# A four-layer convolution network on one core: image halves cut left and right instead of upper and lower, and a ninth-tap pass of 496 columns

## The chip, the cores and the metric

The kernel runs on one core of one Trainium2 chip. The metric is the device time of one execution in microseconds. The kernel before was run three times, 2502.79 to 2504.33 us, with a median of 2503.82 us. One more execution was profiled; times inside the kernel come from that one.

## The reference

The input `x` has the shape (4, 32, 32, 16): batch, rows, columns, channels. Four layers run one after the other, each as `x = x + layer(group_norm(x))`. Layers 0, 1 and 3 are of the kind that matters here:

```python
first = jnp.einsum('ijyx,byxc->bijc', Msq, inputs)
kern = jnp.transpose(G, (0, 1, 5, 4, 2, 3)).reshape(h * w * f, c, 3, 3)
shifted = lax.conv_general_dilated(x_nchw, kern, (1, 1), 'SAME')   # an own 3x3 kernel for each output pixel (i, j)
diff = jax.nn.relu(inputs[:, None, None, :, :, :] - shifted)
second = jnp.einsum('ijyx,bijyxc->bijc', Wsq, diff)
return first - second
```

So for each of the 1024 pixels (i, j) and each of 16 filters the whole 32 x 32 image is convolved with a 3x3x16 kernel of its own (zero padding at the borders), the result is subtracted from the image, clipped at zero and summed with weights. Layer 2 is another one (running maxima over intervals and small matrix products); the change does not touch it.

## The kernel before

**Tiles.** A convolution is a matrix product over 9 taps x 16 channels = 144 rows. The weights of 128 output pixels are the stationary operand, an image is the moving one. The batch is two groups `g` of two images. A *phase* is one group in one of the three convolution layers, so there are six; a phase has 8 *chunks* `t` of 128 pixels, a chunk has 16 filters `f` and 2 images `b`, so there are 6 x 8 x 32 = 1536 *steps*. A *unit* is 4 filters of one chunk: 8 steps share one load of weights.

**Row tiles.** An image is cut into two halves `h` of 512 pixels. Half 0 goes through rows 0 to 63 of the matrix engine, half 1 through rows 64 to 127, at the same time, and they write two PSUM banks. 64 rows hold four taps of 16 channels, so two row blocks (`s` = 0, 1) hold eight taps; the ninth tap, the one a row below and a column to the right, has a block of its own (`im9` with the weights `W9`; the 64 rows hold it four times for the precision scheme). Values are split in a high and a low part (`iy`, `iz`, `iyz`, weights `WU`, `WL`, `WD`), to reach fp32 precision with matmuls in fp32r. A step has 7 *passes*: two with `iy`, two with `iz`, two with `iyz`, and one with `im9`; a pass is a pair of matmuls of 64 rows x 128 columns of weights and 512 columns of image, one on each row tile. `products` (line 581) issues them (line 590). The first 16 steps (`u < PLAIN`) are simpler: two passes in full fp32 straight from the tile `raw`, which count as four in the trace, and the `im9` pass.

**Order.** All queues are written out by hand. `conv_layer` goes through the steps: `first_part` of step i (four passes, then ScalarE scales the bank pair, line 620), then `second_part` of step i-1 (three passes, then VectorE's clip, weighting and sum in one instruction, line 636). Four bank pairs rotate. Between the steps two generators insert other work: `prep_parts` makes the weight parts of the next units (VectorE, ScalarE, GpSimd, then two copies on SyncE's queue from one half of the partitions to the other, line 239, which the second pass of a unit's first step is the first to need), and `behind(phase)` makes the input of the next phase: group norm, then `before_conv` (line 340 on). There the normalized image `xn` is transposed into `xt`, written to the DRAM tile `xs` with a border of zeros (line 352, four transfers), and read back as shifted copies, one for each tap and half, into `raw` (line 361, 24 transfers); then it is split into `iy`, `iz`, `iyz`, `im9` (`split`, `halve`, `difference`). SyncE's queue carries the weight loads `raw<-in_g` (line 107), `WT<-in_w` (113), the copies `parts<-parts` (239) and these transfers, in one order.

**Layout before.** Half `h` is the upper or lower 16 rows of 32 columns; the padded image is 34 wide. The ninth tap reads a row below: the last row of the lower half reads zeros, in the upper half it does not.

**Start.** The first phase gets its shifted images from the host (`xi`, line 143). `kept` (line 746 on) holds for each row of the engine and each border whether it is a tap that looks outside; `normal` normalizes `raw`, and `sides` (line 796) then sets the borders to zero by multiplying with `kept`.

Of the kernel before, what the change touches and what calls it, by code (L numbers as in the profile page):

```python
# [8 lines left out]
F32 = mybir.dt.float32  # L9
# [6 lines left out]
P = 128  # L16
# [5 lines left out]
NP = H * H  # L22
NT = NP // P
HP = H + 2
NPP = HP * HP
HI = H // 2
PITCH = HI * HP
NH = HI * H
RUN = (HI - 1) * HP + H
ROWS = P // H  # L30
FU = 4
NU = C // FU
# [9 lines left out]
def net_kernel(ctx: ExitStack, tc: tile.TileContext, x, xq, xi, convs, iv_w, iv_b, out):  # L42
# [73 lines left out]

    raw = const.tile([P, 3, GB, PITCH], F32, name="raw")
    const.tile([P, 32], F32, name="pad")  # L120
# [4 lines left out]
    const.tile([P, 112], F32, name="pad_parts")  # L125


    F0 = 2
# [46 lines left out]
            dst, src, mask[:, 0:1], dst.bitcast(F32), op0=ALU.mult, op1=ALU.add  # L175
        )

    xs = [dram.tile([GC, NPP], F32, name=f"xs{g}") for g in range(NG)]
    zero = const.tile([P, HP], F32, name="zero")
    xt = [const.tile([P, NT, HP], F32, name=f"xt{g}") for g in range(NG)]  # L180

    def zeros(g):

        nc.gpsimd.memset(xt[g], 0.0)
        for y in (0, HP - 1):
            nc.gpsimd.dma_start(xs[g][:, y * HP : (y + 1) * HP], zero[:GC])

    def image(v, x):
        return v.rearrange("... (y x) -> ... y x", x=x)[..., :H]

    def upper(src, n, name):

        t = work.tile([P, 2, NH], F32, tag="upper", bufs=2, name=f"upper_{name}")[:, :n]
        t = t.rearrange("p s (y x) -> p s y x", x=src.shape[3])
        nc.vector.tensor_scalar(  # L195
            t.bitcast(I32), src.bitcast(I32), HIGH, None, op0=ALU.bitwise_and
        )
        return t.rearrange("p s y x -> p s (y x)")
# [58 lines left out]

    def split(eng, g, b, name, pause=IDLE):

        high = upper(image(raw[:, :2, b], HP), 2, f"x{name}{b}")  # L260
        yield 1
        for s in range(2):
            eng.tensor_tensor(
                image(iz[g][:, s, b], H), image(raw[:, s, b], HP), image(high[:, s], H), ALU.subtract
            )
            yield pause
            nc.scalar.activation(iy[g][:, s, b], high[:, s], AF.Copy, scale=EPS)  # L267
# [72 lines left out]
    def before_conv(g, layer):  # L340
        xn = work.tile([P, NT, GC], F32, tag="xn", bufs=2, name=f"xn_{g}_{layer}")
        xns[g] = xn
        yield from group_norm(g, f"c{g}{layer}", xn, 1 if layer == 2 else 4)

        nc.vector.transpose(
            xt[g][:, :, 1 : 1 + H], xn
        )
        inner = xs[g][:, HP : HP + H * HP].rearrange("p (t r n) -> p r t n", r=ROWS, n=HP)  # L350
        for r in range(ROWS):
            nc.sync.dma_start(inner[:, r], xt[g][GC * r : GC * (r + 1)])
        yield 2
        xsv = xs[g].rearrange("(b c) n -> c b n", b=GB)
        for slot, row, tap in [(tap // 4, tap % 4, tap) for tap in range(8)] + [
            (2, row, 8) for row in range(4)
        ]:
            for h in range(2):
                off = (HI * h + tap // 3) * HP + tap % 3
                r0 = 64 * h + C * row  # L360
                nc.sync.dma_start(
                    raw[r0 : r0 + C, slot ^ h if slot < 2 else 2, :, :RUN], xsv[:, :, off : off + RUN]
                )
            yield 1
        yield 6 if layer == 2 else 12
        for b in range(GB):
            yield from split(nc.gpsimd, g, b, f"{g}{layer}")
            yield IDLE
            halve(image(im9[g][:, b], H), image(raw[:, 2, b], HP), low_x)
            for s in range(2):  # L370
                difference(nc.gpsimd, g, b, s)
            yield 3
            halve_rest(image(im9[g][:, b], H), image(raw[:, 2, b], HP), low_x)
            yield 1

    def load_first_terms(layer):
# [204 lines left out]
        yield 1  # L581


    def products(ps, pairs, first):


        for k, (w, v) in enumerate(pairs):
            for h in range(2):
                r = slice(64 * h, 64 * h + 64)
                nc.tensor.matmul(  # L590
                    ps[:, h, :],
                    lhsT=w[r],
                    rhs=v[r],
                    start=first and k == 0,
                    stop=k == len(pairs) - 1,
                    skip_group_check=not first,
                )

    def first_part(step):
        phase, t, f, b = step  # L600
        g = phases[phase][0]
        n = phase * NT + t
        u = n * NU + f // FU
        ps = bank_pair(f"pc_{n}_{f}_{b}")
        if u < PLAIN:
            products(
                ps,
                [(raws[u][:, s, f % FU], image(raw[:, s, b], HP)) for s in range(2)]
                + [(units[u][3][:, f % FU], im9[g][:, b])],
                True,  # L610
            )
# [8 lines left out]
        nc.scalar.activation(ps, ps, AF.Copy, scale=1.0 + EPS)  # L620
        return ps

    def second_part(step, ps):
# [5 lines left out]
        if u >= PLAIN:  # L629
            WU, WL, WD, W9 = (w[..., f % FU, :] for w in units[u])  # L630
            products(
                ps, [(WD[:, s], iyz[g][:, s, b]) for s in range(2)] + [(W9, im9[g][:, b])], False
            )
        col = b * C + f
        junk = work.tile([P, NP], F32, tag="junk", name=f"junk_{n}_{col}")
# [92 lines left out]
    for b in range(GB):  # L728
# [6 lines left out]
    )  # L735

    outside = {
        "left0": (rows[:, 0, 0::3], rows[:, 1, 2:3]), "right0": (rows[:, 0, 2:3], rows[:, 1, 1:2]),
        "top0": (rows[:, 0, 0:3],), "bottom0": (rows[:, 1, 2:4],),
        "left1": (rows[:, 0, 2:3], rows[:, 1, 0::3]), "right1": (rows[:, 0, 1:2], rows[:, 1, 2:3]),  # L740
    }
    kept = const.tile([P, len(outside) + 4], F32, name="kept")
    keep = {}
    for k, (name, views) in enumerate(outside.items()):
        keep[name] = kept[:, k : k + 1]
        nc.vector.tensor_reduce(keep[name], views[0], axis=AX.X, op=ALU.add)
        if len(views) > 1:
            also = kept[:, len(outside) + k % 4 : len(outside) + k % 4 + 1]
            nc.vector.tensor_reduce(also, views[1], axis=AX.X, op=ALU.add)
            nc.vector.tensor_tensor(keep[name], keep[name], also, ALU.add)  # L750
    kept = kept[:, : len(outside)]
# [43 lines left out]

    def sides(eng, b, slot):

        v = raw[:, slot, b].rearrange("p (y x) -> p y x", x=HP)
        if slot == 2:
            eng.memset(v[:, :, H - 1 : H], 0.0)  # L800
            eng.memset(v[64:, HI - 1, :H], 0.0)
        for side, at in (
            ("left", v[:, :, 0]), ("right", v[:, :, H - 1]),
            ("top", v[:, 0, :H]), ("bottom", v[:, HI - 1, :H]),
        ):
            if f"{side}{slot}" in keep:
                eng.tensor_scalar_mul(at, at, keep[f"{side}{slot}"])  # L807
# [15 lines left out]
    normal(nc.vector, 0, 1)  # L823
    sides(nc.vector, 0, 1)
    sides(nc.gpsimd, 0, 2)
    halve(image(im9[0][:, 0], H), image(raw[:, 2, 0], HP), low_x)
    halve_rest(image(im9[0][:, 0], H), image(raw[:, 2, 0], HP), low_x)
    prep_plain(0, F0, FU, nc.vector)

    def rest_of_start():  # L830

        nc.sync.dma_start(X[0], x[0])
        load_raw(2)
        load_raw(3)
        prep_plain_rest(0, F0, FU)
        for slot in (0, 1, 2):
            normal(nc.vector, 1, slot)
            sides(nc.vector, 1, slot)
        halve(image(im9[0][:, 1], H), image(raw[:, 2, 1], HP), low_x)
        prep_plain(1)  # L840
        prep(2)
        yield 1
        halve_rest(image(im9[0][:, 1], H), image(raw[:, 2, 1], HP), low_x)
# [12 lines left out]
        yield from group_norm(0, "c00", xns[0], 4)  # L856
# [82 lines left out]
```

## Time and profile before

| | |
|---|---|
| three runs, median | 2503.82 us |
| the profiled execution, whole | 2503.48 us |
| its span (first to last instruction) | 2501.8 us |
| granted clock of the matrix engine | 1.0 |
| TensorE matmul (PE) busy | 99% of the span |
| weight load (PEld) busy | 83% |
| VectorE (DVE) busy | 83% |
| ScalarE (ACT) busy | 75% |
| GpSimd (POOL) busy | 44% |
| DMA engines busy | about half of the span |

Everything outside the span is 2503.48 - 2501.8 = 1.7 us. A line of a group reads: line of the kernel, engine, operation, output<-inputs, shapes, count | busy time in us, mean duration of one in ns | idle time of the engine just before them, and what ended most of it. PE is the matmul itself, PEld the weight load, SPq SyncE's queue of transfers. "64\*128 64x512" is a matmul with 64 rows and 128 columns of weights and 512 columns of moving data. Matmuls are pipelined, so the duration of one is longer than the distance from one to the next.

### The profile page before, as it was taken

The page shows a single profiled execution, that of the slowest core. Times are in us where ns is not written, and L with a number is a line of the kernel's source. Part 1 is how long each engine was busy: PE and PEld are TensorE (multiplying, and loading weights), DVE is VectorE, ACT ScalarE, POOL GpSimd, SP SyncE. Part 2 cuts the span into 40 slices and gives each one's busy share as a digit, 9 for nine tenths or more (in the row PEclk, how much of TensorE's full clock was granted, in tenths as well). Part 3 has the DMA queues.
Part 4 walks back from the last instruction along what each step waited for, and adds up shares of the span by engine and source line. Part 5 has one row for each costly group of instructions (what it writes and reads, how often), then busy time and mean ns, then how long its engine had stood idle before and what let it go on. Part 6 is the DMA issues. An engine that isn't in the chain of part 4 may idle for free.

```text
span 2501.8 us, 56663 instructions
## 1 busy us (share of the span) xinstructions
PE 2485.7 (99%) x21906; PEld 2077.8 (83%) x21906; DVE 2078.6 (83%) x3620; ACT 1884.8 (75%) x2181; POOL 1102.3 (44%) x991
## 2 busy tenths in 40 slices
PE   8999999999999999999999999999999999999999
PEld 5899888888888887888888888888889888888887
DVE  8888777888888887888888988888889887788887
ACT  4777777787777777777777777787777777777776
POOL 3445333454343435433345555454646444333332
PEclk9999999999999999999999999999999999999999
DMA  5556444465444664544454444554444467354442
GB/s 174 185 148 171 121 136 140 118 171 140 133 139 134 200 163 123 140 133 133 133 144 136 136 119 138 144 159 133 124 137 137 133 167 203 112 144 136 135 136 54
DMA packets 81182, 353.80 MB, mean 141 GB/s; under 512 B 18448, under 2 KB 20368, under 8 KB 80144
## 3 DMA queue, kind: packets, MB, share of 16 engines
q1 hardware_dynamic: 79920, 349.57, 49.8%
q8 instruction: 172, 2.82, 0.5%
q14 instruction: 98, 0.80, 0.1%
q10 hardware_dynamic: 864, 0.58, 0.1%
q0 software_dynamic: 128, 0.02, 0.0%
HBM read 199.19 MB, written 0.98 MB: 80 GB/s over the span
## 4 chain that ended last, share of the span: by engine, by line
PE 97%; DMA 1%; DVE 1%; issue 1%; ACT 1%; SPq 0%; POOL 0%; ACTq 0%; DVEq 0%; POOLq 0%
PE pc L590 95%; DMA parts<-parts 1%; PE pf L389 1%; DVE junk L636 0%; ACT pc L620 0%; PE ps_l L512 0%; PE ps_r L525 0%; DVE tables L472 0%; ACT parts L232 0%; ACT iy L267 0%; ACT L325 0%; ACT L555 0%; SPq L239 0%; DVE raw L807 0%; PE ps_y L576 0%
## 5 line engine op out<-in xcount | busy, mean ns | idle before, releaser
L636 DVE SCALAR_TENSOR_TENSOR junk<-pc,WT 128x1024 f32<-128x1024 f32 x1536 | 1879.9, 1224 | 398.6 <-PE pc L590 351.0
L620 ACT ACTIVATE pc<-pc 128x1024 f32<-128x1024 f32 x1520 | 1531.9, 1008 | 583.5 <-PE pc L590 549.8
L590 PE MATMUL pc<-iy,parts 64*128 64x512 f32 x6080 | 955.7, 388 | 1.3 <-DMA parts<-parts 1.0
L590 PE MATMUL pc<-iyz,parts 64*128 64x512 f32 x6080 | 953.6, 387 | 2.2 <-ACT pc L620 2.1
L590 PE MATMUL pc<-iz,parts 64*128 64x512 f32 x6080 | 952.7, 387 | 0.0
L590 PEld LDWEIGHTS pc<-iy,parts 64*128 64x128 f32 x6080 | 589.6, 184 | 112.6 <-issue 4.4
L590 PEld LDWEIGHTS pc<-iyz,parts 64*128 64x128 f32 x6080 | 589.2, 184 | 111.1 <-ACT pc L620 6.3
L229 POOL TENSOR_TENSOR parts<-raw,upper_w 128x512 fp32r<-128x512 f32 x190 | 246.0, 1295 | 985.5 <-PE pc L590 817.0
L590 PEld LDWEIGHTS pc<-iz,parts 64*128 64x128 f32 x6080 | 591.1, 184 | 105.1
L590 PE MATMUL pc<-im,W 64*128 64x512 f32 x3072 | 620.0, 391 | 0.0
L590 PEld LDWEIGHTS pc<-im,W 64*128 64x128 f32 x3072 | 301.0, 184 | 56.7 <-issue 3.6
L230 POOL TENSOR_TENSOR W<-W,raw 128x512 fp32r<-128x512 f32 x190 | 247.8, 1304 | 1.9 <-ACT W L171 1.6
L233 POOL TENSOR_TENSOR parts<-parts 128x512 fp32r<-128x512 f32 x190 | 247.2, 1301 | 2.5 <-ACT parts L228 2.4
L206 POOL TENSOR_TENSOR raw<-raw,ident 128x512 f32<-128x512 f32 x190 | 201.9, 1063 | 54.6 <-DMA raw<-in_g 49.3
L171 ACT ACTIVATE W<-raw,low_w 128x512 fp32r<-128x512 f32 x190 | 136.1, 716 | 1.0 <-DMA raw<-in_g 1.0
L636 DVE DVE_READ_ACCUMULATOR junk<-pc,WT 128x1 f32 x1536 | 127.8, 83 | 0.0
L228 ACT ACTIVATE parts<-upper_w 128x512 fp32r<-128x512 f32 x190 | 118.7, 625 | 3.4 <-DVE upper_w L195 3.3
L232 ACT CAST parts<-upper_w 128x512 fp32r<-128x512 f32 x190 | 116.8, 615 | 0.0
L195 DVE TENSOR_SCALAR upper_w<-raw 128x512 int32<-128x512 int32 x190 | 82.2, 433 | 0.2
L651 POOL TENSOR_SCALAR acc<-acc 128x32 f32<-128x32 f32 x40 | 11.5, 288 | 159.3 <-DVE junk L636 155.2
L544 POOL TENSOR_TENSOR tables<-ft_b,rt 128x1089 f32<-128x1089 f32 x16 | 37.7, 2356 | 0.1
L544 POOL TENSOR_TENSOR tables<-ft_a,rt 128x1089 f32<-128x1089 f32 x16 | 37.6, 2350 | 0.0
(140 smaller groups left out, 393.5 us busy)
## 6 DMA issues: line engine op xcount, KB each, us to landing
raw<-in_g SPq DMA_DIRECT2D x190, 768.0 KB, 7.0
parts<-parts SPq DMA_DIRECT2D x380, 384.0 KB, 4.9
WT<-in_w SPq DMA_DIRECT2D x48, 512.0 KB, 4.8
MT<-in_mt SPq DMA_DIRECT2D x6, 2048.0 KB, 14.3
raw<-xs SPq DMA_DIRECT2D x120, 67.8 KB, 2.5
raw<-in_xi SPq DMA_DIRECT2D x3, 271.0 KB, 4.6
raw<-in_xi SPq DMA_DIRECT2D x1, 813.0 KB, 7.0
xs<-xt SPq DMA_DIRECT2D x20, 34.0 KB, 2.1
```

The source lines that it names most:

```text
L171: nc.scalar.activation(dst, src, AF.Copy, scale=mask[:, 1:2])
L195: nc.vector.tensor_scalar(t.bitcast(I32), src.bitcast(I32), HIGH, None, op0=ALU.bitwise_and)
L206: eng.tensor_tensor(raws[u][:, s, at:to], raws[u][:, s, at:to], pick[s][:, f0 + at : f0 + to].unsqueeze(2).to_broadcast([P, to - at, P]), ...
L228: nc.scalar.activation(WD, high, AF.Copy, scale=-EPS)
L229: nc.gpsimd.tensor_tensor(WL, w8, high, ALU.subtract)
L230: nc.gpsimd.tensor_tensor(W9, W9.bitcast(F32), src[:, 2], ALU.add)
L232: nc.scalar.copy(WU, high)
L233: nc.gpsimd.tensor_tensor(WD, WD.bitcast(F32), WL.bitcast(F32), ALU.add)
L544: nc.gpsimd.tensor_tensor(t, ft[:, i, :].unsqueeze(1).to_broadcast([P, T1, T1]), rt, ALU.add,)
L590: nc.tensor.matmul(ps[:, h, :], lhsT=w[r], rhs=v[r], start=first and k == 0, stop=k == len(pairs) - 1, skip_group_check=not first,)
L620: nc.scalar.activation(ps, ps, AF.Copy, scale=1.0 + EPS)
L636: nc.vector.scalar_tensor_tensor(junk, ps.rearrange("p h n -> p (h n)"), 0.0, chunks[n], op0=ALU.min, op1=ALU.mult, accum_out=accs[phase][ ...
```

## The change

The halves become left and right: half `h` holds 32 rows of columns 16 h to 16 h + 15. The padded half is 34 rows of `WP` = 18 columns. The ninth tap looks one row down, so in both halves the last of the 32 rows reads only the border's zeros; its pass leaves out these 16 columns on both row tiles (`n = LAST` = 31 x 16 = 496 instead of 512). What else follows from the layout: `raw` holds 574 instead of 542 elements for each tap and image, in runs of 16 of 18 instead of 32 of 34; `xs` keeps both halves with their own border columns, so line 352 writes it in eight transfers with rows of 18 instead of four with rows of 34; the 24 transfers of line 361 read 574 elements in a run. At the start `kept` takes 8 reductions instead of 10 reductions and 4 additions, `sides` multiplies four borders of slot 1 instead of two, and clears one strip of slot 2 instead of two. Two unused tiles are resized and `raw` moves behind `im9`. The host orders `in_w` and `xi` for the new halves. Order and number of all other instructions stay as they are.

```diff
-HI = H // 2
-PITCH = HI * HP
-NH = HI * H
-RUN = (HI - 1) * HP + H
+HW = H // 2
+WP = HW + 2
+PITCH = H * WP
+NH = H * HW
+RUN = (H - 1) * WP + HW
+LAST = (H - 1) * HW
...
-    xs = [dram.tile([GC, NPP], F32, name=f"xs{g}") for g in range(NG)]
+    xs = [dram.tile([GC, 2, HP * WP], F32, name=f"xs{g}") for g in range(NG)]
...
     def image(v, x):
-        return v.rearrange("... (y x) -> ... y x", x=x)[..., :H]
+        return v.rearrange("... (y x) -> ... y x", x=x)[..., :HW]
...
-        inner = xs[g][:, HP : HP + H * HP].rearrange("p (t r n) -> p r t n", r=ROWS, n=HP)
+        inner = xs[g][:, :, WP : WP + H * WP].rearrange("p h (t r n) -> p h r t n", r=ROWS, n=WP)
         for r in range(ROWS):
-            nc.sync.dma_start(inner[:, r], xt[g][GC * r : GC * (r + 1)])
+            for h in range(2):
+                nc.sync.dma_start(
+                    inner[:, h, r], xt[g][GC * r : GC * (r + 1), :, HW * h : HW * h + WP]
+                )
...
             for h in range(2):
-                off = (HI * h + tap // 3) * HP + tap % 3
+                off = tap // 3 * WP + tap % 3
                 r0 = 64 * h + C * row
                 nc.sync.dma_start(
-                    raw[r0 : r0 + C, slot ^ h if slot < 2 else 2, :, :RUN], xsv[:, :, off : off + RUN]
+                    raw[r0 : r0 + C, slot ^ h if slot < 2 else 2, :, :RUN], xsv[:, h, :, off : off + RUN]
                 )
...
-    def products(ps, pairs, first):
+    def products(ps, pairs, first, ninth=False):
         for k, (w, v) in enumerate(pairs):
+            n = LAST if ninth and k == len(pairs) - 1 else NH
             for h in range(2):
                 r = slice(64 * h, 64 * h + 64)
                 nc.tensor.matmul(
-                    ps[:, h, :],
+                    ps[:, h, :n],
                     lhsT=w[r],
-                    rhs=v[r],
+                    rhs=v[r] if n == NH else v[r][:, :n],
...
-        "left0": (rows[:, 0, 0::3], rows[:, 1, 2:3]), "right0": (rows[:, 0, 2:3], rows[:, 1, 1:2]),
-        "top0": (rows[:, 0, 0:3],), "bottom0": (rows[:, 1, 2:4],),
-        "left1": (rows[:, 0, 2:3], rows[:, 1, 0::3]), "right1": (rows[:, 0, 1:2], rows[:, 1, 2:3]),
+        "left0": rows[:, 0, 0::3], "right0": rows[:, 1, 1:2],
+        "top0": rows[:, 0, 0:3], "bottom0": rows[:, 1, 2:4],
+        "left1": rows[:, 0, 2:3], "right1": rows[:, 1, 2:3],
+        "top1": rows[:, 1, 0:3], "bottom1": rows[:, 0, 2:4],
```

More of the change, by code (lines that the diff above doesn't have):

```diff
@@ L24 @@
 HP = H + 2
-NPP = HP * HP
-HI = H // 2
-PITCH = HI * HP
-NH = HI * H
-RUN = (HI - 1) * HP + H
+HW = H // 2
[4 more added lines that the diff above has]
+LAST = (H - 1) * HW
 ROWS = P // H
@@ L113, in load_chunk @@
             nc.sync.dma_start(chunks[n], convs[phases[n // NT][1]][1][t * P : (t + 1) * P, :])
-    raw = const.tile([P, 3, GB, PITCH], F32, name="raw")
-    const.tile([P, 32], F32, name="pad")
+    const.tile([P, 224], F32, name="pad")
     iy = [const.tile([P, 2, GB, NH], F32R, name=f"iy{g}") for g in range(NG)]
@@ L124, in net_kernel @@
     im9 = [const.tile([P, GB, NH], F32R, name=f"im9{g}") for g in range(NG)]
-    const.tile([P, 112], F32, name="pad_parts")
+    raw = const.tile([P, 3, GB, PITCH], F32, name="raw")
+    const.tile([P, 120], F32, name="pad_parts")
     F0 = 2
@@ L176, in halve_rest @@
         )
-    xs = [dram.tile([GC, NPP], F32, name=f"xs{g}") for g in range(NG)]
-    zero = const.tile([P, HP], F32, name="zero")
+    xs = [dram.tile([GC, 2, HP * WP], F32, name=f"xs{g}") for g in range(NG)]
+    zero = const.tile([P, 2 * WP], F32, name="zero")
     xt = [const.tile([P, NT, HP], F32, name=f"xt{g}") for g in range(NG)]
@@ L185, in zeros @@
         for y in (0, HP - 1):
-            nc.gpsimd.dma_start(xs[g][:, y * HP : (y + 1) * HP], zero[:GC])
+            nc.gpsimd.dma_start(
+                xs[g][:, :, y * WP : (y + 1) * WP], zero[:GC].rearrange("p (h n) -> p h n", h=2)
+            )
     def image(v, x):
-        return v.rearrange("... (y x) -> ... y x", x=x)[..., :H]
+        return v.rearrange("... (y x) -> ... y x", x=x)[..., :HW]
     def upper(src, n, name):
@@ L258, in split @@
     def split(eng, g, b, name, pause=IDLE):
-        high = upper(image(raw[:, :2, b], HP), 2, f"x{name}{b}")
+        high = upper(image(raw[:, :2, b], WP), 2, f"x{name}{b}")
         yield 1
@@ L263, in split @@
             eng.tensor_tensor(
-                image(iz[g][:, s, b], H), image(raw[:, s, b], HP), image(high[:, s], H), ALU.subtract
+                image(iz[g][:, s, b], HW), image(raw[:, s, b], WP), image(high[:, s], HW), ALU.subtract
             )
@@ L349, in before_conv @@
         )
-        inner = xs[g][:, HP : HP + H * HP].rearrange("p (t r n) -> p r t n", r=ROWS, n=HP)
+        inner = xs[g][:, :, WP : WP + H * WP].rearrange("p h (t r n) -> p h r t n", r=ROWS, n=WP)
         for r in range(ROWS):
-            nc.sync.dma_start(inner[:, r], xt[g][GC * r : GC * (r + 1)])
+            for h in range(2):
+                nc.sync.dma_start(
+                    inner[:, h, r], xt[g][GC * r : GC * (r + 1), :, HW * h : HW * h + WP]
+                )
         yield 2
-        xsv = xs[g].rearrange("(b c) n -> c b n", b=GB)
+        xsv = xs[g].rearrange("(b c) h n -> c h b n", b=GB)
         for slot, row, tap in [(tap // 4, tap % 4, tap) for tap in range(8)] + [
@@ L368, in before_conv @@
             yield IDLE
-            halve(image(im9[g][:, b], H), image(raw[:, 2, b], HP), low_x)
+            halve(image(im9[g][:, b], HW), image(raw[:, 2, b], WP), low_x)
             for s in range(2):
@@ L372, in before_conv @@
             yield 3
-            halve_rest(image(im9[g][:, b], H), image(raw[:, 2, b], HP), low_x)
+            halve_rest(image(im9[g][:, b], HW), image(raw[:, 2, b], WP), low_x)
             yield 1
@@ L607, in first_part @@
                 ps,
-                [(raws[u][:, s, f % FU], image(raw[:, s, b], HP)) for s in range(2)]
+                [(raws[u][:, s, f % FU], image(raw[:, s, b], WP)) for s in range(2)]
                 + [(units[u][3][:, f % FU], im9[g][:, b])],
-                True,
+                True, ninth=True,
             )
@@ L631, in second_part @@
             products(
-                ps, [(WD[:, s], iyz[g][:, s, b]) for s in range(2)] + [(W9, im9[g][:, b])], False
+                ps, [(WD[:, s], iyz[g][:, s, b]) for s in range(2)] + [(W9, im9[g][:, b])],
+                False, ninth=True,
             )
@@ L737, in net_kernel @@
     outside = {
-        "left0": (rows[:, 0, 0::3], rows[:, 1, 2:3]), "right0": (rows[:, 0, 2:3], rows[:, 1, 1:2]),
-        "top0": (rows[:, 0, 0:3],), "bottom0": (rows[:, 1, 2:4],),
-        "left1": (rows[:, 0, 2:3], rows[:, 1, 0::3]), "right1": (rows[:, 0, 1:2], rows[:, 1, 2:3]),
+        "left0": rows[:, 0, 0::3], "right0": rows[:, 1, 1:2],
+        "top0": rows[:, 0, 0:3], "bottom0": rows[:, 1, 2:4],
+        "left1": rows[:, 0, 2:3], "right1": rows[:, 1, 2:3],
+        "top1": rows[:, 1, 0:3], "bottom1": rows[:, 0, 2:4],
     }
-    kept = const.tile([P, len(outside) + 4], F32, name="kept")
+    kept = const.tile([P, len(outside)], F32, name="kept")
     keep = {}
-    for k, (name, views) in enumerate(outside.items()):
+    for k, (name, view) in enumerate(outside.items()):
         keep[name] = kept[:, k : k + 1]
[L746 to L751, printed above, removed]
+        nc.vector.tensor_reduce(keep[name], view, axis=AX.X, op=ALU.add)
     nc.vector.tensor_scalar(kept, kept, -1.0, 1.0, op0=ALU.mult, op1=ALU.add)
@@ L796, in sides @@
     def sides(eng, b, slot):
-        v = raw[:, slot, b].rearrange("p (y x) -> p y x", x=HP)
+        v = raw[:, slot, b].rearrange("p (y x) -> p y x", x=WP)
         if slot == 2:
-            eng.memset(v[:, :, H - 1 : H], 0.0)
-            eng.memset(v[64:, HI - 1, :H], 0.0)
+            eng.memset(v[64:, :, HW - 1 : HW], 0.0)
         for side, at in (
-            ("left", v[:, :, 0]), ("right", v[:, :, H - 1]),
-            ("top", v[:, 0, :H]), ("bottom", v[:, HI - 1, :H]),
+            ("left", v[:, :, 0]), ("right", v[:, :, HW - 1]),
+            ("top", v[:, 0, :HW]), ("bottom", v[:, H - 1, :HW]),
         ):
@@ L825, in net_kernel @@
     sides(nc.gpsimd, 0, 2)
-    halve(image(im9[0][:, 0], H), image(raw[:, 2, 0], HP), low_x)
-    halve_rest(image(im9[0][:, 0], H), image(raw[:, 2, 0], HP), low_x)
+    halve(image(im9[0][:, 0], HW), image(raw[:, 2, 0], WP), low_x)
+    halve_rest(image(im9[0][:, 0], HW), image(raw[:, 2, 0], WP), low_x)
     prep_plain(0, F0, FU, nc.vector)
@@ L838, in rest_of_start @@
             sides(nc.vector, 1, slot)
-        halve(image(im9[0][:, 1], H), image(raw[:, 2, 1], HP), low_x)
+        halve(image(im9[0][:, 1], HW), image(raw[:, 2, 1], WP), low_x)
         prep_plain(1)
@@ L842, in rest_of_start @@
         yield 1
-        halve_rest(image(im9[0][:, 1], H), image(raw[:, 2, 1], HP), low_x)
+        halve_rest(image(im9[0][:, 1], HW), image(raw[:, 2, 1], WP), low_x)
         prep_plain_rest(1)
@@ L879 @@
     give("xq", xc.reshape(GB, C, 4, 256).transpose(2, 0, 1, 3).reshape(P, 256))
-    xp = np.pad(xc, ((0, 0), (0, 0), (1, 1), (1, 1))).reshape(GB, C, NPP)
+    xp = np.pad(xc, ((0, 0), (0, 0), (1, 1), (1, 1)))
     xi = np.zeros((GB, 2, 3, 4, C, PITCH), np.float32)
@@ L883 @@
         for tap in range(9):
-            off = (HI * h + tap // 3) * HP + tap % 3
+            off = tap // 3 * WP + tap % 3
             rows = slice(None) if tap == 8 else tap % 4
             slot = 2 if tap == 8 else tap // 4 ^ h
-            v = xp[:, :, off : off + RUN]
+            v = xp[..., HW * h : HW * h + WP].reshape(GB, C, HP * WP)[:, :, off : off + RUN]
             xi[:, h, slot, rows, :, :RUN] = v[:, None] if tap == 8 else v
@@ L893 @@
         give(f"mt{n}", m.transpose(3, 5, 4, 1, 0, 2).reshape(2, P, NT // 2, 4, 256))
-        give(f"w{n}", a[f"{pre}_{w}"].reshape(NP, NP))
+        give(f"w{n}", a[f"{pre}_{w}"].reshape(NP, H, 2, HW).transpose(0, 2, 1, 3).reshape(NP, NP))
         g = a[f"{pre}_G"].reshape(NT, P, 9 * C, NU, FU).transpose(0, 3, 2, 4, 1)
```

## The prediction, made before the changed kernel was run

> **What bounds the kernel now.** I read the profile's page first: engines, the chain that ended last, the groups of instructions.
>
> ```profile
> PE 2485.7 (99%) x21906; PEld 2077.8 (83%) x21906; DVE 2078.6 (83%) x3620; ACT 1884.8 (75%) x2181; POOL 1102.3 (44%) x991
> ...
> L636 DVE SCALAR_TENSOR_TENSOR junk<-pc,WT 128x1024 f32<-128x1024 f32 x1536 | 1879.9, 1224 | 398.6 <-PE pc L590 351.0
> L620 ACT ACTIVATE pc<-pc 128x1024 f32<-128x1024 f32 x1520 | 1531.9, 1008 | 583.5 <-PE pc L590 549.8
> L590 PE MATMUL pc<-iy,parts 64*128 64x512 f32 x6080 | 955.7, 388 | 1.3 <-DMA parts<-parts 1.0
> ...
> L590 PE MATMUL pc<-im,W 64*128 64x512 f32 x3072 | 620.0, 391 | 0.0
> L590 PEld LDWEIGHTS pc<-im,W 64*128 64x128 f32 x3072 | 301.0, 184 | 56.7 <-issue 3.6
> ```
>
> PE is busy 99% of the span and idles next to nothing before its groups; VectorE and ScalarE idle mostly for PE. The chain gives PE 97%. A step costs VectorE 1224 + 83 ns and ScalarE 1008 ns, and how long it lasts is read from PE's timeline in the middle of the run (start, length, count):
>
> ```profile
> 1001.10 0.39 PE L590 MATMUL pc<-im,W 64*128 64x512 f32 x2
> 1001.33 0.62 PE L590 MATMUL pc<-iy,parts 64*128 64x512 f32 x4
> 1001.78 0.62 PE L590 MATMUL pc<-iz,parts 64*128 64x512 f32 x4
> 1002.24 0.62 PE L590 MATMUL pc<-iyz,parts 64*128 64x512 f32 x4
> 1002.69 0.39 PE L590 MATMUL pc<-im,W 64*128 64x512 f32 x2
> ```
>
> From one ninth-tap pass to the next 1.59 us: seven passes of 227 ns, the two row tiles side by side. Over all steps the distance is 1.587 us almost everywhere; 1536 of them would be 2438 us. So a pass that becomes shorter shortens the run, if columns and not weights set its 227 ns, and if nothing else falls due earlier than it is ready.
>
> **Part 1: 16 columns less in each ninth-tap pass.** Both tiles must shorten, and both do. Is 227 ns a price by column? No fp32r pass of fewer columns is in the trace, but the interval layer has fp32 matmuls of three lengths on the same 64x128 tile, from the view of groups that keeps shapes apart:
>
> ```profile
> L525 PE MATMUL ps_r<-tables,r 64*128 64x352 f32 x8 | 3.0, 454 | 0.0
> L525 PE MATMUL ps_r<-tables,r 64*128 64x231 f32 x8 | 2.2, 358 | 0.0
> L525 PE MATMUL ps_r<-tables,r 64*128 64x110 f32 x8 | 1.5, 261 | 0.0
> ```
>
> (454 - 261) / 242 = 0.80 ns per column, the same over both steps. The plain steps' fp32 passes of 512 columns follow each other at 428 ns, fp32r ones at 227, so fp32r streams twice as fast: 0.40 ns per column, 6.4 ns for 16. From the other side, if all of the 227 ns goes by columns, 227 / 512 x 16 = 7.1 ns. I take 6.65, between them. Times 1536: **-10.2 us** (bounds -9.8 and -10.9).
>
> Could the weight load hold the pass at 227? The load of the next pass starts with the pass and lasts 184 ns; 220 still leaves 36. The 231-column passes start 198 ns apart with a load of 185 between. So I take no floor above 198 ns, and keep "no gain" as a rival.
>
> The Trainium skill, "TensorE: Matmul & The Clock Gate", section "Back-to-back issue gap", states for streams of load and matmul a sustained 81 ns per matmul at 128 columns and 131 at 512. That slope, 0.13 ns per column and matmul, makes an estimate of 4.2 ns per pair and 6.4 us in all; its 131 x 2 = 262 ns for a pair stands against the 227 measured here, so I do not follow it.
>
> VectorE, ScalarE and the other passes keep their sizes; at 1.580 us a step VectorE's 1.307 still fits.
>
> **Part 2: SyncE's queue in the five preparations.** The eight transfers at line 352 stand where four did, ahead of everything later in the queue. At phase 5, in SyncE's timeline:
>
> ```profile
> 2014.49 2.01 SPq L352 DMA_DIRECT2D xs<-xt  x4
> 2018.28 2.63 SPq L361 DMA_DIRECT2D raw<-xs  x6
> 2021.02 1.11 SPq L239 DMA_DIRECT2D parts<-parts  x2
> 2022.17 1.90 SPq L107 DMA_DIRECT2D raw<-in_g  x1
> 2024.11 10.93 SPq L361 DMA_DIRECT2D raw<-xs  x16
> 2035.52 1.16 SPq L239 DMA_DIRECT2D parts<-parts  x2
> ```
>
> One issue takes 0.45 us (median of line 352; 0.33 to 0.75), so four more push what follows back by D = 1.8 us. Pieces are 72 instead of 136 bytes, 256 to a transfer as before. Landing is 2.1 us for 256 pieces of line 352 and 2.5 for the 32 long ones of line 361, so pieces cost little, and I add nothing. What is late: weight copies `parts<-parts`, behind these transfers. Landing of the last copy against the unit's first matmul, for that phase:
>
> ```profile
> DMA to landing us min/median/max: 4.9/5.5/6.1
> 2042.76 0.62 PE L590 MATMUL pc<-iy,parts 64*128 64x512 f32 x4
> ```
>
> Issued 2036.05, landed 6.1 later at 2042.16, used at 2042.76: 0.6 us to spare, and 0.23 more, since only the second pass reads the copied rows. The same sum in the other preparations: 208.77 - 205.88 = 2.9; 520.67 - 518.25 = 2.4; 927.14 - 925.59 = 1.55; 1628.28 - 1627.17 = 1.1. A push of 1.8, and 0.12 for 18 steps that are 6.65 ns shorter, against these plus 0.23: late by 0, 0, 0.1, 0.6, 1.1 us. PE then waits: +1.8 us. After the two waits of this kind that the run has (at 131 and 2093 us) the next two steps are 0.07 and 0.04 longer, three times 0.1: **+2.1 us in all**.
>
> At phase 4 the last shifted image lands at 1631.0 and VectorE takes it at 1631.27; it will wait about a microsecond there. A step's sum may be 1.7 us late before PE misses its bank pair (used again 3.17 us after the step ends, 1.47 needed), so I put 0. If it were wrong, below 1 us. The 6% longer `raw` transfers, the runs of 16 of 18 in GpSimd's and VectorE's work on the images (20 instructions of 1.2 us, GpSimd idle 56%) lie beside PE: 0. Weights and images move by whole steps of 512 bytes in the program's addresses, and weights at all such steps are read at the same 1.587 us now: 0.
>
> "DMA: Bandwidth & Descriptors", section "Specifications", says that transfers below 512 B are read, modified and written; it speaks against 72-byte rows, but 136 is below it too, and no run here shows the difference.
>
> **Part 3: the start.** The 14 `kept` instructions take 2.73 to 4.25 us, on the chain. Three reductions in a row take 0.27, each after the first some 0.06, so eight take 0.6: -0.9. What they release, the sum over `XQ`, has its data at 0.81 + 2.4 = 3.2. The two more borders of slot 1 (four of them take 0.81) come before the third pass: +0.4. Of the rest a tenth goes to a weight transfer landing at 6.5. **-0.4 us**, bounds -1 (all of the first, borders hidden) and +1 (the images, 6% more bytes, late).
>
> **Sum.** -10.2 + 2.1 - 0.4 = -8.5 against the profiled execution's 2503.48 us: **2495.0 us**. That execution lies 0.3 below the median of the runs, so the change from the median would be -8.8.
>
> **The rivals.**
>
> *The pass does not shorten* (the change does not do what it says): something outside the columns, such as weight load to matmul, holds 227 ns. For it: 512 columns at 0.40 ns are 205 ns, and 22 of the 227 stay unexplained. Against: the 198 ns. Time: 2503.5 + 2.1 - 0.4 = 2505.2.
>
> *The copies wait longer; slower.* Place: line 352 on SyncE's queue. With c us per issue instead of 0.45, D = 8c - 1.8. Past D = 3 all five preparations stall, sum 5 x (D + 0.12) less the 9.7 us to spare. At c = 0.6 (D = 3) it is 5.9 us, time about 2499. At 0.71 it eats the whole gain, from 0.84 on the kernel is slower by over 0.2%; at c = 1, D = 6.2, it is 22 us of waits and about 2515. For it: the slowest of the 20 issues took 0.75, and slow landing adds to D. Against: the median, and landing within 3.3 us in all 20.
>
> *No stall at all* (issues overlap with waits the queue has anyway): 2503.5 - 10.2 - 0.4 = 2492.9, down to 2491.6 with the far bounds.
>
> **How the numbers follow.** Under 0.2% (5 us) a measurement of this kernel can hardly tell from no change. Forecast with 0 to 5 us of stalls, the last rival inside it, 2491 to 2498.5: 0.70. Longer stalls that leave part of the gain, or a lower price per column, 2498.5 to 2503: 0.15, more than half of it under 2501, and half counted as faster. Pass not shortened: 0.09. Slower: 0.06. The range 2491 to 2501 holds about 0.8; the far side of c lies outside it. Faster 0.78, same 0.16, slower 0.06.
>
> **What would show it.** Steps of 1.580 instead of 1.587 us in PE's timeline, the `im,W` group at 496 columns and some 6 ns shorter. Line 352 eight times, about 3.6 us. PE waiting for `parts<-parts` near 1628 and 2042 us, up to 1 us each. First plain matmul near 9.0 instead of 9.8 us. Steps of 1.587 would make part 1 wrong; waits in the first two preparations, part 2.

## The result, and the profile after

The changed kernel took 2495.93 us (median of eight runs, 2494.64 to 2497.89), the kernel before on the same chip 2503.06 us (eight runs, 2502.32 to 2504.33): a ratio of 0.9972 with a 95% interval of 0.9961 to 0.9983, 7.1 us faster. Measured twice more on other chips, beside the kernel before, the same kernel gave 0.9976 (0.9966 to 0.9985; 2497.53 us) and 0.9975 (0.9964 to 0.9986; 2496.67 us). The forecast was 2495.0 us, 8.5 less than the profiled execution of before.

The profiled execution took 2497.43 us; its span is 2495.7 us, 6.1 us shorter than before's. First the page's engines and groups:

```profile
PE 2478.2 (99%) x21906; PEld 2080.4 (83%) x21906; DVE 2081.2 (83%) x3617; ACT 1882.6 (75%) x2181; POOL 1103.0 (44%) x990
...
L597 PE MATMUL pc<-iy,parts 64*128 64x512 f32 x6080 | 957.3, 387 | 3.8 <-DMA parts<-parts 3.2
...
L597 PE MATMUL pc<-im,W 64*128 64x496 f32 x3072 | 609.5, 384 | 0.0
```

PE is still busy 99%. The `im,W` group has 496 columns on both tiles and 384 instead of 391 ns. The `iy` group, whose idle time was 1.3 us with 1.0 for `parts<-parts`, now has 3.8 with 3.2: the weight copies are late in more places. PE's timeline in the middle of the run:

```profile
1000.97 0.38 PE L597 MATMUL pc<-im,W 64*128 64x496 f32 x2
1001.18 0.62 PE L597 MATMUL pc<-iy,parts 64*128 64x512 f32 x4
...
1002.54 0.38 PE L597 MATMUL pc<-im,W 64*128 64x496 f32 x2
```

From one ninth-tap pass to the next it is 1.57 us here, in rounded numbers. From the unrounded records, the mean over all undisturbed steps (about 1430 of 1535 distances) went from 1.5867 to 1.5800 us, 6.67 ns less; times 1535 that is 10.2 us. So some 4 us came back elsewhere. Laid side by side step by step, the two runs differ, beyond the 6.67 ns, in a few places: at the start, near 520, 914 to 927 and 2042 us, where PE waits for `parts<-parts`, and at 131 and 2093 us, where it did so before already.

SyncE's timeline in the preparation at 900 us (the third of five) shows what stands ahead of the copies, first before, then after:

```profile
903.63 1.80 SPq L352 DMA_DIRECT2D xs<-xt  x4
905.60 2.29 SPq L239 DMA_DIRECT2D parts<-parts  x2
907.93 0.59 SPq L107 DMA_DIRECT2D raw<-in_g  x1
908.69 11.16 SPq L361 DMA_DIRECT2D raw<-xs  x16
920.01 1.10 SPq L239 DMA_DIRECT2D parts<-parts  x2
```

```profile
900.04 4.15 SPq L356 DMA_DIRECT2D xs<-xt  x8
904.35 1.10 SPq L242 DMA_DIRECT2D parts<-parts  x2
905.50 1.20 SPq L108 DMA_DIRECT2D raw<-in_g  x1
906.81 11.78 SPq L367 DMA_DIRECT2D raw<-xs  x16
918.76 1.11 SPq L242 DMA_DIRECT2D parts<-parts  x2
```

Eight writes to `xs` (line 356 now), the copies for one unit, the load `raw<-in_g`, sixteen shifted images, the copies for the next unit. The chain of what ended last runs through this queue here, which it did not before:

```profile
905.50 9.04 DMA raw<-in_g
914.54 0.02 issue
914.56 0.30 SPq L367
...
919.27 6.40 DMA parts<-parts
...
925.71 2.35 PE pc L597 x15
```

Read it so: the load landed after 9.04 us; only then SyncE issued the next image, nine of them one after the other, then the copies; the second copy took 6.40 us to land, and PE had been waiting for it. Two steps of it were not in the prediction: that the queue stands still until the load has landed, and the 6.40.

The start, PE's timeline of before, then of after:

```profile
9.80 3.75 PE L590 MATMUL pc<-raw,first 64*128 64x512 f32 x8 [1.99 <-DVE raw L807]
12.60 1.20 PE L590 MATMUL pc<-im,W 64*128 64x512 f32 x2
13.63 1.88 PE L590 MATMUL pc<-raw,first 64*128 64x512 f32 x8
14.94 0.80 PE L590 MATMUL pc<-im,W 64*128 64x512 f32 x2
```

```profile
8.93 3.81 PE L597 MATMUL pc<-raw,first 64*128 64x512 f32 x8 [2.03 <-DVE raw L810]
...
12.95 2.57 PE L597 MATMUL pc<-raw,first 64*128 64x512 f32 x8
14.96 0.79 PE L597 MATMUL pc<-im,W 64*128 64x496 f32 x2
```

The first plain matmul comes 0.87 us earlier, but the second `im` pass is at the same time. The second set of eight `raw` matmuls lasts 2.57 instead of 1.88 us: in the records its passes start 0.85 us apart until 14.5 us and 0.43 from then on, in the run before 0.43 already from 13.6 us. The matmuls ran at half speed for 0.9 us longer. The trace's first record of the granted clock (1.0) stands at 13.4 us before and at 14.3 us after, and in all twelve profiles of this study it stands where the distances halve.

VectorE lost time behind that. It sets the borders of the second image, two in slot 1 before and four after:

```profile
14.85 0.39 DVE L807 TENSOR_SCALAR raw<-raw,kept 128x16 f32<-128x16 f32 x2
```

```profile
14.68 2.39 DVE L810 TENSOR_SCALAR raw<-raw,kept 128x32 f32<-128x32 f32 x4
```

Two of the four take 1.0 to 1.1 us instead of 0.25, and each of the two ends 0.03 to 0.05 us after the operation of GpSimd that runs beside it (1.04 us). All ten profiles with the new layout have one or two such borders here, and the two with the old layout none; no run moves GpSimd's work away, so that it is the cause stays unproven. VectorE's first clip starts at 17.8 instead of 16.0 us.

### The profile page after: what moved, and what is told of

Same layout as the page of the kernel before. It is cut to its first block, busy times and chain, and to the rows that moved or that the text cites. A ratio compares the mean times of both kernels' runs of the same rounds, so it can differ in the third digit from the quotient of the medians.

```text
span 2495.7 us, 56685 instructions
## 1 busy us (share of the span) xinstructions
PE 2478.2 (99%) x21906; PEld 2080.4 (83%) x21906; DVE 2081.2 (83%) x3617; ACT 1882.6 (75%) x2181; POOL 1103.0 (44%) x990
## 4 chain that ended last, share of the span: by engine, by line
PE 95%; DMA 2%; DVE 1%; SPq 1%; issue 1%; ACT 1%; POOL 0%; DVEq 0%; ACTq 0%; POOLq 0%
PE pc L597 94%; DMA parts<-parts 1%; PE pf L395 1%; DMA raw<-in_g 1%; DVE junk L644 1%; SPq L367 0%; ACT pc L627 0%; SPq L356 0%; SPq L242 0%; PE ps_r L531 0%; PE ps_l L518 0%; DVE tables L478 0%; DMA xs<-xt 0%; ACT iy L270 0%; ACT L328 0%
## 5 line engine op out<-in xcount | busy, mean ns | idle before, releaser
L597 PE MATMUL pc<-im,W 64*128 64x496 f32 x3072 | 609.5, 384 | 0.0
```

The lines of the kernel that those rows point to most:

```text
L597: nc.tensor.matmul(ps[:, h, :n], lhsT=w[r], rhs=v[r] if n == NH else v[r][:, :n], start=first and k == 0, stop=k == len(pairs) - 1, skip_g ...
```

## The experiments

The theory: the gain is the 16 columns; the loss is the four more transfers in SyncE's queue, which push the weight copies behind them. Rivals: the gain is the layout's (A); the copies are late because faster steps need them earlier, whatever the queue does (B). Ratios are against the kernel before on the same chip. "The changed kernel" is the one of the result, edits are against it unless another is named.

**1. The columns alone.** Against the kernel before:

```diff
+            n = 496 if ninth and k == len(pairs) - 1 else NH
...
-                    ps[:, h, :],
+                    ps[:, h, :n],
...
-                    rhs=v[r],
+                    rhs=v[r] if n == NH else v[r][:, :n],
```

> The columns alone: the kernel before with its upper and lower halves, and the ninth tap's pass cut to 496 columns on both row tiles; it leaves out the ninth tap for the last 16 pixels of each half. Line 352 stays at four transfers. Theory (the gain is the 16 columns, the loss is the four more transfers on SyncE's queue): steps of 1.580 us, the waits of the kernel before and no others, 2503.1 - 10.25 = 2492.8 us, 2492 to 2494. Rival A (the gain is the layout's, not the columns'): steps of 1.587, 2503 us. Rival B (the added waits come because the run is faster, its weight copies due earlier, and not from the queue): steps of 1.580, and the waits of the changed kernel here too, about 2496 us.

Measured: 2493.94 us against 2504.01, ratio 0.9962 (0.9950 to 0.9975), 10.1 us less. Steps of 1.5800 us. PE's only wait of over 0.15 us for the copies is the one near 2093 us (2088 here), where before had one too:

```profile
PE pc L591 <- DMA parts<-parts: 0.9, 1, 0.9
```

It waits for them in none of the five preparations: the ones that were late by 1.6 us near 927 and by 1.3 near 2042 us in the changed kernel are in time by 1.9 and 1.35 here. A falls, and B falls too: the steps are as fast and nothing is late.

**2. The layout alone.**

```diff
-LAST = (H - 1) * HW
+LAST = NH
```

> The layout alone: the changed kernel with all 512 columns in the ninth tap's pass; nothing is left out. Theory: steps of 1.587 us, PE's waits for parts<-parts in the preparations as in the changed kernel, 2503.1 + 3 = 2506 us, 2504.5 to 2508.5. Rival A (the layout gives the gain): 2496 us. Rival B (the waits come from the faster steps): 2503 us, waits as in the kernel before.

Measured: 2506.98 us, ratio 1.0014 (1.0004 to 1.0023), 3.0 us more than before. Steps of 1.5867 us, those of before, and waits for the copies near 520, 914, 927 and 2042 us of 0.4, 0.5, 1.4 and 1.8 us, in the distances of steps: at the changed kernel's places, with before's steps.

```profile
PE pc L597 <- DMA parts<-parts: 3.6, 3, 1.4
```

(The view counts gaps of over 0.15 us between PE's records, which are shorter than the loss in the distances, and has the wait near 2093 us in it.)

Not all of the loss is the copies: in this profile PE also lost 1.4 us between 15 and 45 us, where VectorE was late with its first clips. The two halves of the change add up, -10.1 + 3.0 = -7.1 us, within intervals that reach about 3.1 and 2.4 us to each side.

**3. Half of the writes on another queue.** The layout and the columns stay; SyncE has four writes as before.

```diff
-                nc.sync.dma_start(
+                (nc.gpsimd if h else nc.sync).dma_start(
                     inner[:, h, r], xt[g][GC * r : GC * (r + 1), :, HW * h : HW * h + WP]
```

> The changed kernel with four of its eight xs<-xt transfers (those of the right half) on GpSimd's queue, so that SyncE issues four as before. Theory: the 1.8 us push is gone; PE's waits for parts<-parts near 520, 914 to 927 and 2042 us are gone or under 0.3 us each, steps of 1.580, about 2493.5 us, 2492.5 to 2495. Rival B (the waits come from the faster steps, or from the landing of the transfers and not from their place in the queue): as the changed kernel, about 2496 us.

Measured: 2493.37 us, ratio 0.9962 (0.9950 to 0.9975). SyncE's timeline in the third preparation of this kernel:

```profile
899.45 1.81 SPq L356 DMA_DIRECT2D xs<-xt  x4
901.42 1.11 SPq L242 DMA_DIRECT2D parts<-parts  x2
...
916.06 1.10 SPq L242 DMA_DIRECT2D parts<-parts  x2
```

The first copies stand 2.0 us behind the first write (4.3 in the changed kernel), the second ones 16.6 (18.7), and PE waits for neither. Repeated beside the changed kernel on one chip:

> The changed kernel with four of its eight xs<-xt transfers on GpSimd's queue, again, beside the changed kernel on one chip. Theory: 2.5 to 4 us faster than the changed kernel, about 2493 us, and no wait for parts<-parts in the preparations. Rival (the difference of the first time was that of two chips): within 1 us of the changed kernel.

2494.15 us (2493.09 to 2496.41, five runs; ratio 0.9964, 0.9950 to 0.9977) against 2497.53 (2494.08 to 2500.72, nine runs): 3.4 us. The two intervals overlap a little (0.9964, up to 0.9977, and 0.9976, from 0.9966); the waits, which are gone in both profiles, say the same as the times. It is the fastest version of this study that computes all of it, and its ratio is that of the columns alone.

**4. All of the writes on GpSimd's queue.**

```diff
-                nc.sync.dma_start(
+                nc.gpsimd.dma_start(
                     inner[:, h, r], xt[g][GC * r : GC * (r + 1), :, HW * h : HW * h + WP]
```

> The changed kernel with all eight xs<-xt transfers on GpSimd's queue, so that SyncE issues none there, 1.8 us less than the kernel before. Theory: PE's waits for parts<-parts in the preparations gone, about 2493 us, no better than with four on each queue by more than 0.7. Rival C (eight issues on GpSimd take so long that the images, the splits or GpSimd's own weight work come late): new waits, over 2495 us. Rival B: about 2496 us.

Measured: 2498.86 us, ratio 0.9984 (0.9975 to 0.9993): rival C's side, in part by the way it named. What SyncE's queue waited for between 899 and 930 us:

```profile
SPq L367 <- DMA xs<-xt: 8.2, 2, 4.9
```

In preparations 2 and 3 the eight writes, issued 0.58 us apart on GpSimd beside a load that SyncE now issued at once, land 4.8 to 7.5 us after issue instead of 1.6 to 2.4. In the other three they land after 1.9 us as a rule (one took 3.1), but the eighth goes out 4.1 us after the first and has landed 6.0 to 7.2 us after it, against 3.5 to 4.3 in the kernel before and 5.1 to 5.6 in the changed one; that is rival C as it stands. Either way the images that read `xs` wait on SyncE, and the copies behind the images with them: waits near 927, 1628 and 2042 us of 1.3, 1.2 and 1.2 us. Taking the writes off the queue helps only while the last of them lands as soon.

**5. The suspected price doubled.**

```diff
-                nc.sync.dma_start(
-                    inner[:, h, r], xt[g][GC * r : GC * (r + 1), :, HW * h : HW * h + WP]
-                )
+                for part in range(2):
+                    c = slice(GC // 2 * part, GC // 2 * (part + 1))
+                    nc.sync.dma_start(
+                        inner[c, h, r], xt[g][GC * r : GC * (r + 1), :, HW * h : HW * h + WP][c]
+                    )
```

> The changed kernel with each of its eight xs<-xt transfers cut in two by partitions: sixteen issues on SyncE, of 9 KB and 128 pieces of 72 bytes each, the same bytes in all. Theory (price by issue, 0.45 us each): line 356 lasts 7.2 us instead of 3.6, everything behind it is pushed by 3.6 more, and from the slack of the weight copies in the changed kernel (+1.6, -0.6, -1.6, +0.8, -1.3 us in preparations 1 to 5) PE waits 2.0, 4.2, 5.2, 2.8 and 4.9 us: some 15 us more than the changed kernel, about 2511 us, 2506 to 2514. Rival (the price goes by pieces or bytes, which stay the same): line 356 lasts 3.6 us, 2496 us.

Measured: 2515.19 us (2512.47 to 2519.71), ratio 1.0049 (1.0037 to 1.0062), 17.7 more than the changed kernel on that chip. SyncE's timeline of it at the third preparation, and PE's waits:

```profile
908.63 8.22 SPq L358 DMA_DIRECT2D xs<-xt  x16
```

```profile
PE pc L599 <- DMA parts<-parts: 12.9, 10, 2.2
```

The sixteen took 7.4 to 8.2 us; by issue, not by bytes. The waits by preparation, in the distances of steps: 2.5, 5.4, 4.8, 2.8 and 4.2 us, 19.6 in all, against 19.1 expected. That nearness is in part luck: in preparations 2 and 3, after PE had idled 3.0 and 2.4 us for the copies, the granted clock stood at 0.5 for 3.41 us (from 514.43 and from 924.03 us), and half of that time, 1.7 us each, is in the 5.4 and 4.8.

```profile
514.50:517.80 3.30, 3.30 (x18) 2.58 (x18) 1.23 (x2) 1.59 (x2) 0.84 (x1) 0.50 0.67 181
```

(Busy time of PE, PEld, VectorE, ScalarE and GpSimd in that stretch, then the granted clock, 0.50, and the DMA engines' share and GB/s.) The copies alone cost some 16.2 us. The time came out just above the expected range; in this profile the first plain matmul comes at 10.0 us and the full clock at 16.1, and the second `im` pass 1.4 us later than in the changed kernel's.

**6. The load taken out of the queue.** The records show that a transfer of SyncE is issued only after the eighth one before it has landed (in the changed kernel all of some 790 pairs after 30 us, the closest by 0.02 us; they count on eight semaphores in turn). So the eighth transfer after `raw<-in_g` has to wait for its landing: seven images go out, and nine are left. One load per preparation goes elsewhere:

```diff
-            load_raw(u + RAWS)
+            load_raw(u + RAWS, nc.gpsimd if u in (14, 38, 70, 124, 156) else nc.sync)
```

> The changed kernel, its eight xs<-xt transfers left on SyncE; only the 768 KB load raw<-in_g that stands between the two pairs of weight copies of each preparation (once in each of the five) is issued on GpSimd's queue. Theory: on SyncE every transfer waits for the landing of the eighth before it, so the ninth transfer after this load waits until the load has landed, and the second unit's copies are issued 4.2 us after that landing in every profile so far; without the load in SyncE's sequence they come 3 us or more earlier than in the changed kernel (by +14 to +16 instead of +18.4 to +18.7 us after the first xs write in preparations 2 and 3), and PE's waits near 520, 914 to 927 and 2042 us are gone: about 2493.5 us, 2492.5 to 2495. Rival (a push by issues alone): the copies come earlier by the one issue taken away, 1.2 us; about half of the waits of preparations 3 and 5 stay, 2495 to 2497 us. Second rival (the load lands late on GpSimd's queue, behind its work): waits of GpSimd for raw, and a slower kernel than the changed one.

Measured: 2499.85 us, ratio 0.9987 (0.9978 to 0.9996), slower than the changed kernel (2496.67 on that chip). Half of the theory held: the second unit's copies came 16.3 and 16.4 us after the first write in preparations 2 and 3 (18.4 and 18.7 in the changed kernel; 14 to 16 expected), and in all five preparations they were in time. The other half did not: the first unit's copies, in the changed kernel's first profile in time or late by at most 0.6, were late by 1.2, 0.1, 0.9, 2.9 and 1.8 us; behind the 2.9 the granted clock stood at 0.5 for 3.41 us, which is another 1.7. The transfers of this kernel between 900 and 909 us:

```profile
raw<-in_g POOLq DMA_DIRECT2D x1, 768.0 KB, 5.8
parts<-parts SPq DMA_DIRECT2D x2, 384.0 KB, 6.2
xs<-xt SPq DMA_DIRECT2D x8, 18.0 KB, 5.4
```

On its own queue the load starts at 900.82, in the midst of the writes, and these take 5.4 instead of 1.8 us to land; the images wait for them. That is neither rival: the load is not late, it is too early. In the changed kernel, the queue's order had kept it behind the writes. The Trainium skill says in "DMA: Bandwidth & Descriptors", section "Issuing engines are not separate DMA queues", that transfers from all issuing engines run on the same 16 DMA engines and that another issuer saves only the issuing time. Experiments 4 and 6 agree (writes beside a load land after 4.8 to 7.5 and 5.4 us instead of 1.8); experiment 3 shows that the issuing time alone can be worth 3.4 us where something urgent stands behind it.

**7. The changed kernel again, twice.**

> The changed kernel once more, unchanged, on the chip of the next three. Theory: 2496 us; PE's waits for parts<-parts at the same places (520, 914 to 927, 2042 us). The start: first plain matmul at 8.9 us again, but the time at which the passes halve to 0.43 us differs by up to 1 us, as the granted clock rises at a time of its own. Rival to the reading of preparation 3 (the second copies of 905 and 919 us landed 6.5 instead of 5.1 us after issue by chance): 5.1 us this time, and the wait at 927 us 1.3 us shorter. If it is the 16 KB instruction packet that falls beside them, it falls there again, since both follow the program: 6.4 to 6.6 us again.

> The changed kernel a third time, unchanged, on the chip of the run before it. Theory: 2496 to 2498 us; PE's waits near 914 and 927 us of 2.2 us together, as in both profiles so far, since their copies have an instruction packet beside them each time; those near 520 and 2042 us present or not, as they lie within a microsecond of the point where the copies are in time. Rival (the waits at 914 and 927 us are as chancy as the others): they are missing or of another size here.

The waits near 914 and 927 us are there both times (together 2.1 and 2.7 us; 2.2 in the first profile), with second copies that land 6.4 to 7.2 us after issue. The others are chance: 0.5, 0 and 0.35 us near 520, and 1.2, 0 and 0 near 2042 us. Half-speed passes ended at 14.5, 14.5 and 13.5 us.

Why 6.4 and not 5.1? The view of transfers shows, for the time from 919.3 us, the issue, to 925.6 us, just before the landing in the changed kernel, a packet of the instruction queue:

```profile
q8 instruction: 1, 0.02, 1.0%
...
parts<-parts SPq DMA_DIRECT2D x1, 384.0 KB, 6.4
```

and for the same copy in experiment 1, from 916.5 to 921.6 us, none beside the queue of the program's own transfers:

```profile
q1 hardware_dynamic: 248, 1.11, 91.0%
...
parts<-parts SPq DMA_DIRECT2D x1, 384.0 KB, 5.1
```

Of these packets 172 have 16 KB and take 1.0 us on one of the 16 DMA engines, and 98 have 8 KB and take 0.36. Over the whole run of the changed kernel: of the second copies that landed within 8 us, 24 took over 5.7 us, and every one had an instruction packet started between 0.5 us before and 5 us after its issue; of the 157 normal ones (5.07 median), 35 had. In the kernel before: 25 of 25, and 33 of 158; in experiment 2, 22 of 23. In experiment 5 the second copies of the third preparation landed in 5.1 us; no packet is beside the first of them, and one starts 4.5 us after the issue of the other, 0.6 us before it lands. I could not move a packet alone, so this is a coincidence seen in these traces, not a test.

**8. How far the price by column holds.**

```diff
-LAST = (H - 1) * HW
+LAST = 256
```

> The changed kernel with 256 instead of 496 columns in the ninth tap's pass; it leaves out the ninth tap for the lower half of the rows. It asks how far the price by column (6.65 ns for 16) holds. By columns all the way: 240 x 0.417 = 100 ns less per step, 1.480 us, about 2342 us. With the weight load of 184 ns as a floor (a pass of 184 to 198 ns instead of 220): steps of 1.544 to 1.558 us, 22 to 36 ns less, about 2441 to 2463 us. I take the floor: the load of 184 ns was no bound at 220 ns, but is longer than the 120 ns that 256 columns would take.

Measured: 2410.7 us, ratio 0.9629 (0.9612 to 0.9647); steps of some 1.507 us, 73 ns less, where I had taken 22 to 36 by a floor and 100 without one. Both were wrong. In PE's records the short pass itself went from 220 to 116 ns, 0.43 ns per column and far below the 184 ns of a weight load, so the load is no floor for one pass; but the other six passes went from 227 to 231 to 235 ns each, which takes some 30 ns back. Why those grew stays open. The granted clock is not why: it was 1.00 from 1000 to 2000 us, and the passes have the same lengths there. The loads that must catch up are one candidate; another sign is that the two row tiles of a pass start a median of 37 ns apart, where it is 3 in the changed kernel. PE's idle time tells the rest:

```profile
L597 PE MATMUL pc<-iy,parts 64*128 64x512 f32 x6080 | 1031.4, 395 | 15.0 <-DMA parts<-parts 11.2
```

With shorter steps the copies are late in nine places, for 11.2 us, and three times the granted clock stood at 0.5 for 3.41 us behind such a wait.

## Why the prediction was right, and where it was not

By its own steps, in us against the profiled run of before; the last three columns are the three profiles of the changed kernel:

| step | forecast | first | second | third |
|---|---|---|---|---|
| 16 columns, all steps | -10.2 | -10.2 | -10.2 | -10.2 |
| waits, preparation 1 | 0 | 0 | 0 | 0 |
| preparation 2 | 0 | +0.5 | 0 | +0.35 |
| preparation 3 | +0.1 | +2.2 | +2.1 | +2.7 |
| preparation 4 | +0.6 | 0 | 0 | 0 |
| preparation 5, re-sync | +1.4 | +1.2 | 0 | 0 |
| start, up to the second `im` pass | -0.4 | 0.0 | 0.0 | -0.6 |
| the rest | 0 | +0.5 | -1.1 | +0.4 |
| to the last step | -8.5 | -5.8 | -9.2 | -7.3 |

**The columns: right, in mechanism and size.** 6.65 ns per pass forecast, 6.67 measured in three profiles and, within 0.1, in experiments 1, 3 and 5. Experiment 2 takes it away alone and 1 brings it alone. The slope from the three fp32 lengths, halved, was enough; the unexplained 22 ns per pass stayed with the pass, as assumed. The Trainium skill gives in the section that the prediction drew on also an isolated gap of N / 2.4 + 2.5 ns; its slope makes 6.67 ns of 16 columns, as measured, while the sustained figures' slope of 4.2 is refuted here. Its constant does not fit: 512 columns make an estimate of 215.8 ns by it, 226.7 are measured per pair of tiles.

**The push: right as a mechanism, mis-sized where it falls.** Experiments 1, 2, 3 and 5 all show it: it goes with the four transfers and grows with their number, at 0.43 to 0.45 us per issue. The step that failed is "a push of 1.8, and 0.12 for 18 steps ... against these": one delay for all five preparations. By the prediction's own signs ("waits in the first two preparations" would make part 2 wrong) it failed in part: PE waited in the second preparation in two of three profiles, and near 1628 us, where a wait was forecast, in none. From the first write to the second unit's copies, the delay was in fact +1.1, +2.9, +2.3, 0.0 and +2.8 us. In four of the five preparations these copies are issued 4.2 us after the landing of `raw<-in_g`, before and after, because the queue waits there and nine images follow; so what counts is when that load lands. In preparation 4 it landed at the same distance from the first write (17.5 us), and the push vanished in waits the queue had anyway; VectorE did not wait there for the shifted image either, as I had forecast it would. In preparation 2 the load took 9.1 instead of 8.2 us to land, and the push grew. In preparation 3 the landing beside an instruction packet adds 1.3 to 2.1 us, every time. Over- and underestimates partly cancelled, which is luck: 2.1 forecast, 3.9, 2.1 and 3.1 measured.

**The start: the head start came, and was mostly lost again.** The first plain matmul was forecast near 9.0 instead of 9.8 us and came at 8.9, 9.1 and 8.9 us in the three profiles. The term of +0.4 for two more borders before the third pass did not show: the first `im` pass is as much earlier as the first matmul (0.84 and 0.87 us in the first profile). What the sum lacked is the clock. The passes run at half speed until the granted clock is 1.0, and half of a head start that is spent at half speed is lost. This moment lies between 12.6 and 16.1 us in the twelve profiles, 3.2 to 6.1 us after the first plain matmul; with one start, that of before, it is 13.4 us in the kernel before and 15.4 in experiment 1. The rest of the head start is below that spread. Whether an earlier begin moves the moment, no experiment shows.

**The rest.** At 131 and 2093 us the copies share the DMA engines with another large load; there the changed kernel's three runs waited 0.9 to 1.0 us less, and 0.8 and 0.7 more or 0.5 less. Before was no fixed point there, and I had treated it as one. The other part is VectorE's delay at the borders of the second image, for which the prediction has no term: between 15 and 45 us, where its first clips are late, PE lost 0.2, 0.1 and 0.4 us in the three profiles, and 0.6 to 1.4 in experiments 2, 3, 4 and 6.

**The rivals.** "The pass does not shorten" is refuted by experiment 1. "The copies wait longer" is the mechanism that came in part, and its formula came near where it was driven: at sixteen issues, D = 12 x 0.45 = 5.4, it gives 5 x 5.52 - 9.7 = 17.9 us of waits; measured are 19.6, or some 16.2 without the two stretches at half the clock, which the formula does not have. "No stall" is what experiment 3 is: 2492.9 forecast, 2493.37 and 2494.15 measured.

## What to carry to other kernels

Where one engine is busy 99%, what shortens its every step by little is worth its full price, and the price of a few columns could be read from other matmuls of several lengths in the trace. Half of the columns was another matter (experiment 8): other passes grew and the copies were late. What such a change adds elsewhere is to be looked for in the queues: count the issues, see what urgent transfer stands behind them and how late it may be, and ask first what the queue waits for already, since a push disappears in one wait and is passed on by the next. A transfer moved to another queue starts at another time as well; see what it will then run beside.

## What the runs showed of the hardware that I had not expected

A copy of 384 KB that usually lands in 5.07 us took 5.8 to 7.1 us, mostly about 6.4, in 24 cases of the changed kernel's run, and each of the 24 had an instruction packet beside it (as had 35 copies that were not late). This program loads instructions through the same DMA engines all the time: 270 such packets in the changed kernel's run, 3.6 MB.

A pass of 256 columns among passes of 512 takes 116 ns with weight loads of 184 ns: a single short pass was not held by its load here.

The granted clock reached 1.0 between 12.6 and 16.1 us in the twelve profiles, and the first plain matmul came between 8.9 and 10.0 us in kernels with the same start; one profile of each kernel can't tell what a microsecond saved at the start is worth.

A wait can cost more than its length: after 2.0 to 3.2 us of idle time of PE within some 4 us, the granted clock stood at 0.5 for 3.41 us, six times in experiments 5, 6 and 8. One wait of 2.2 us in experiment 5 had no such stretch behind it.

Small operations of VectorE (32 elements on each of 128 partitions) that take 0.22 to 0.26 us elsewhere took 0.9 to 1.1 us beside one of GpSimd of 1.04 us, in all ten profiles with the new layout.
